# Preparation pieces of an attention kernel, split in halves over two odd slots

## The chip, the core and the metric

The kernel runs on one core of a Trainium2 chip. A core has five engines that each work through their own queue in order: TensorE (PE, matmul, with its weight loads as PEld), VectorE (DVE), ScalarE (ACT), GpSimd (POOL) and SyncE (SP, which issues DMAs). They wait for each other by semaphores. The metric is the device time of one launch in microseconds; three runs of the kernel before gave a median of 1124.78 (1123.45 to 1125.7).

## What is computed

One layer of causal attention over 2048 positions of width 512 with 16 heads of 32, and then a mixture of experts with a shared expert. All is float32. Cut to what matters here:

```python
qkv = (x @ w_qkv).reshape(B, S, 3, H, D)             # S = 2048, H = 16, D = 32
q, k, v = qkv[:, :, 0], qkv[:, :, 1], qkv[:, :, 2]
q, k = unit_norm(q), unit_norm(k)                    # per head, over D
q, k = rope_on_every_second_head(q), rope_on_every_second_head(k)
logits = einsum('bshd,bthd->bhst', q, k) * q_gain
attn = softmax(where(causal, logits, lowest))
x = layernorm(x + einsum('bhst,bthd->bshd', attn, v).reshape(B, S, Dm) @ w_out)
x = layernorm(x + experts(x))                        # top 2 of 8 experts, and a shared one
```

## The kernel before

The change lies in `fast_attention`, which takes the first 570 us. It runs under a manual schedule: every engine does its work in the order in which the Python code emits it.

**Units and slots.** The 16 heads make 4 groups g of 4 heads, the queries 4 blocks b of 512, the keys 16 tiles kt of 128. A *unit* is one (g, b, kt) with kt not behind block b: 4 + 8 + 12 + 16 = 40 units a group, 160 in all. The main loop (L518) has one *slot* n for each unit. Within a block, masked (diagonal) and whole key tiles alternate. A masked unit has 512, 384, 256 or 128 columns of queries, by its place on the diagonal; a whole one has 512. In slot n:

- `scores(n)` (L335) issues four matmuls of 32 contraction rows, one for each head of the group, into two pairs of PSUM banks. There are three pairs (`banks(1, 3, 1)`, L521), so the first pair of unit n needs the second exponential of unit n-2 done, and the second pair the first exponential of unit n-1.
- `exps(n, 0)` and `exps(n, 1)` (L350, ScalarE) read one pair each and write probabilities to one of three buffers.
- `sums(n - 1)` (L365, VectorE) adds the probabilities of the unit before to the block's sums. `causal(n)` (L358, GpSimd) masks the diagonal tile of a masked unit.
- `values(n)` (L380, TensorE) multiplies the probabilities with v into the block's one accumulator bank. It is kept back in `pending` and comes in a later slot. The last one of a block lets ScalarE copy the accumulator out (`fy`, L396).

**Other work in the slots.** The preparation of later units comes in *pieces*: `qkv(u, tl)` (L117) makes q, k and v of one tile of 128 positions for one group and block u = 4g + b. A piece has two steps, `first` (two matmuls with 128 rows and 384 columns) and `second` (two more, then two ScalarE copies, L139 and L140, out of PSUM). It needs a bank from the pool "m", which from slot 8 on is a **single bank**. The fourth piece of u starts `norm_rope(u)` (L146), whose six steps are spread over the next six slots: squares (ScalarE), lengths (VectorE), the root's seeds (ScalarE, L626 and L627), scaling (VectorE), and two rotations (VectorE and GpSimd). Then two *short steps* `qk_transposed(u, s)` (L200) turn q and k with four transposes in the same single bank and a ScalarE copy (L211). When a block ends, an *end step* (L402) adds its sums over the partitions with four matmuls (L405), again in the single bank; ScalarE copies them out (L414) and takes Ln and Exp (L415, L416), and VectorE refines and divides (L422 to L428).

**Order by slot parity**, from slot 8 to 159. In an even slot, after the scores, all pending values of earlier units are issued (as a rule two units), and one short step or an end step where one is due. In an odd slot `long_step(n)` (L452) takes the next piece and issues both its steps; the pending values wait for the next even slot. Where `rests(n)` (L477) is true, or `may_start` (L445) finds that the buffers of the next piece are not free, the odd slot goes without a piece: it then issues the values of the unit before, and the next even slot has those of one unit. A group has 20 odd slots and 16 pieces. The odd slots without a piece are 11, 21, 29 and 37 in the first group, 43, 53, 63 and 73 in the second, and 83, 93, 103 and 113 in the third. The fourth group has no pieces left to hand out after slot 127 and takes the output projections instead.

```python
for step in queue.pop(0)[1]:                     # L455, in long_step
    step()
...
if n % 2 and (rests(n) or not long_step(n)):     # L558, in an odd slot
    values_before(n)
```

## Time and profile before

| | us |
|---|---|
| runs, median of 3 | 1124.78 (1123.45 to 1125.7) |
| the profiled execution | 1121.6 |
| its span, first to last instruction | 1119.9 |
| scores of slot 0, 40, 80, 120 start at | 34.6, 175.7, 301.4, 427.7 |
| TensorE busy | 1097.1 |
| VectorE busy | 584.2 |
| ScalarE busy | 511.3 |
| GpSimd busy | 215.7 |

How to read the rows: the first number of a row of the order of time is its start in microseconds from the start of the span, the second its length, then engine, line, operation, out<-in, the shapes and the number of records put together (a matmul of this kernel leaves two records). In square brackets stands the idle time of the engine ahead of it, and what ended it. Matmuls are pipelined and their ends are modelled: the distance from one row's start to the next one's is the safer measure. In the stretches of busy times, the numbers of one row are its length and then the busy time of PE, PEld, DVE, ACT and POOL, each with its count.

### The profile page before, as it was taken

The page shows a single profiled execution, that of the slowest core. Times are in us where ns is not written, and L with a number is a line of the kernel's source. Part 1 is how long each engine was busy: PE and PEld are TensorE (multiplying, and loading weights), DVE is VectorE, ACT ScalarE, POOL GpSimd, SP SyncE. Part 2 cuts the span into 40 slices and gives each one's busy share as a digit, 9 for nine tenths or more (in the row PEclk, how much of TensorE's full clock was granted, in tenths as well). Part 3 has the DMA queues.
Part 4 walks back from the last instruction along what each step waited for, and adds up shares of the span by engine and source line. Part 5 has one row for each costly group of instructions (what it writes and reads, how often), then busy time and mean ns, then how long its engine had stood idle before and what let it go on. Part 6 is the DMA issues. An engine that isn't in the chain of part 4 may idle for free. (4 is left out here: it accounts for less than half of the span.)

```text
span 1119.9 us, 14794 instructions
## 1 busy us (share of the span) xinstructions
PE 1097.1 (98%) x5810; PEld 576.0 (51%) x5810; DVE 584.2 (52%) x771; ACT 511.3 (46%) x858; POOL 215.7 (19%) x249
## 2 busy tenths in 40 slices
PE   9999999999999999999999999999999999999997
PEld 6543333334334344333356677666665656557774
DVE  1467887787877877887865451111111111104445
ACT  3577878777877877757551100121111212111111
POOL 0221222223133221210000011111111110025441
PEclk9999999999999999999999999999999999999998
DMA  9700000000000000062112496311221211035451
GB/s 284 271 1 1 1 1 1 2 1 1 1 1 1 1 1 1 20 232 61 39 67 104 169 324 214 119 66 66 67 66 64 64 61 57 29 128 186 162 158 57
DMA packets 49539, 88.15 MB, mean 79 GB/s; under 512 B 8016, under 2 KB 22352, under 8 KB 49360
## 3 DMA queue, kind: packets, MB, share of 16 engines
q1 hardware_dynamic: 43376, 69.37, 18.2%
q0 software_dynamic: 5280, 17.31, 4.9%
q8 instruction: 49, 0.80, 0.3%
q10 hardware_dynamic: 800, 0.39, 0.1%
q14 instruction: 34, 0.28, 0.1%
HBM read 65.56 MB, written 27.79 MB: 83 GB/s over the span
## 5 line engine op out<-in xcount | busy, mean ns | idle before, releaser
L352 ACT ACTIVATE big<-fps_s,neg_gmax 128x1024 f32<-128x1024 f32 (+3 forms) x320 | 296.9, 984 | 63.8 <-PE fps_s L342 59.4
L378 DVE TENSOR_TENSOR facc<-facc,big 128x2048 f32<-128x2048 f32 (+3 forms) x128 | 248.9, 1945 | 48.1 <-ACT big L352 29.5
L126 PE MATMUL fps_qkv<-big,shared 128*128 128x384 f32 x512 | 181.0, 497 | 1.1 <-ACT big L211 0.8
L342 PE MATMUL fps_s<-big 32*128 32x512 f32 (+3 forms) x1280 | 169.3, 576 | 3.9 <-ACT big L352 2.5
L387 PE MATMUL fps_av<-big 128*32 128x512 f32 (+3 forms) x1280 | 139.7, 536 | 2.1 <-POOL big L363 1.9
L126 PEld LDWEIGHTS fps_qkv<-big,shared 128*128 128x128 f32 x512 | 92.0, 190 | 88.8 <-ACT big L211 14.9
L363 POOL TENSOR_SCALAR_AFFINE_SELECT big<-big 128x512 f32<-128x512 f32 x64 | 72.1, 1127 | 338.6 <-ACT big L352 330.5
L1048 DVE COPY xT<-ps_xT 128x512 f32<-128x512 f32 x32 | 22.1, 691 | 161.4 <-PE ps_xT L1046 161.4
L342 PEld LDWEIGHTS fps_s<-big 32*128 32x128 f32 x1280 | 54.6, 182 | 93.6 <-issue 52.1
L1079 PE MATMUL ps_dr<-big,hT 128*128 128x512 f32 (+3 forms) x240 | 93.4, 593 | 0.5 <-ACT hT L1056 0.5
L1087 ACT COPY y<-ps_dr 128x512 f32<-128x512 f32 x34 | 19.9, 586 | 157.4 <-PE ps_dr L1079 157.4
L1223 PE MATMUL ps_gr<-big,xT 128*128 128x352 f32 (+1 forms) x320 | 86.3, 460 | 0.0
L1223 PE MATMUL ps_ur<-big,xT 128*128 128x352 f32 (+1 forms) x320 | 86.2, 460 | 0.0
L1037 POOL DMA_INDIRECT rows<-x1d,rows_of x34 | 32.5, 955 | 243.3 <-PE ps_xT L1046 198.0
L679 PE MATMUL ps_us<-big,shared 128*128 128x256 f32 x336 | 78.4, 379 | 0.0
L387 PEld LDWEIGHTS fps_av<-big 128*32 128x32 f32 x1280 | 31.8, 108 | 82.7 <-issue 64.8
L1223 PEld LDWEIGHTS ps_gr<-big,xT 128*128 128x128 f32 (+1 forms) x320 | 50.3, 173 | 39.4 <-issue 18.7
L690 ACT ACTIVATE acts<-ps_gs 128x256 f32<-128x256 f32 x34 | 12.9, 379 | 124.6 <-PE ps_gs L679 124.6
L679 PEld LDWEIGHTS ps_us<-big,shared 128*128 128x128 f32 x336 | 63.8, 190 | 8.6
L679 PE MATMUL ps_gs<-big,shared 128*128 128x256 f32 x280 | 66.9, 382 | 0.0
L1004 PE MATMUL ps_ds<-shared,big 128*128 128x512 f32 x140 | 61.6, 594 | 0.6 <-DVE big L692 0.6
L1223 PEld LDWEIGHTS ps_ur<-big,xT 128*128 128x128 f32 (+1 forms) x320 | 48.0, 174 | 22.6 <-issue 2.3
(204 smaller groups left out, 1096.6 us busy)
## 6 DMA issues: line engine op xcount, KB each, us to landing
yd<-y SPq DMA_DIRECT2D x34, 256.0 KB, 2.0
big<-in_L_ffn_w_gate_dram SPq DMA_DIRECT2D x8, 704.0 KB, 10.0
big<-in_L_ffn_w_up_dram SPq DMA_DIRECT2D x8, 704.0 KB, 10.3
big<-in_L_attn_x_dram SPq DMA_DIRECT2D x16, 256.0 KB, 4.6
fres<-in_L_attn_x_dram SPq DMA_DIRECT2D x16, 256.0 KB, 3.0
x1d<-big SPq DMA_DIRECT2D x16, 256.0 KB, 2.0
big<-in_L_ffn_w_down_dram SPq DMA_DIRECT2D x8, 512.0 KB, 7.2
out_dram<-big SPq DMA_DIRECT2D x16, 256.0 KB, 2.0
```

The lines of the kernel that those rows point to most:

```text
L126: nc.tensor.matmul(ps[0], xT[:, t, c * P : (c + 1) * P], wq_sb[c].rearrange("p (s m) -> p s m", s=3)[:, :, g * P : (g + 1) * P], start=(c ...
L342: nc.tensor.matmul(pss[n][i // 2][:, i % 2, off:], k_at[(g * NB + kb) % KV][r, kl, :], q_at[u % Q][r, off:], start=True, stop=True,)
L352: nc.scalar.activation(pr_at[n % PR][:, 2 * j : 2 * j + 2, off:], pss[n][j][:, :, off:], AF.Exp, bias=neg_gmax)
L363: nc.gpsimd.affine_select(d, d, [[0, 4], [1, P]], ALU.is_ge, 0.0, base=0, channel_multiplier=-1)
L378: nc.vector.tensor_tensor(acc[:, :, off:], first[:, :, off:], pr[:, :, off:], ALU.add)
L387: nc.tensor.matmul(avs[g, b][32 * i : 32 * i + 32, off:], v_at[(g * NB + kb) % KV][:, kl, i * HD : (i + 1) * HD], pr_at[n % PR][:, i, off: ...
L679: nc.tensor.matmul(ps.rearrange("p (t m) -> p t m", t=BT), w[:, c, lo : lo + P], x[:, :, c, :], start=(c == 0), stop=(c == NC - 1),)
L1004: nc.tensor.matmul(pd, hid[:, j, tl * P : (tl + 1) * P], wd[:, j, :], start=(j == 0), stop=False)
L1037: nc.gpsimd.indirect_dma_start(r, None, x1d, bass.IndirectOffsetOnAxis(ap=rows_of[:, i : i + 1], axis=0))
L1048: nc.any.tensor_copy(xT, pst)
L1079: nc.tensor.matmul(pd[slots, :], hT[:w, c, slots], big[:w, bass.ds(at_d + (DOWNS + c * DM), DM)], start=(c == 0), stop=(c == NHC - 1),)
L1223: nc.tensor.matmul(ps[slots, :], xT[:, c, slots], big[:, bass.ds(at_e + (at + c * HE), HE)], start=(c == 0), stop=(c == NC - 1),)
```

## The change

`rests` becomes `halved`, which names other slots, and `long_step` gets a flag. Where an odd slot is halved, `long_step` issues only the first step of the next piece and keeps the second in `held`; the next call issues that step and nothing else. While a step is held, the even slot between the two issues neither a short step nor an end step, since the single bank is occupied. No odd slot rests any more by rule.

```diff
+        held = []
+
-        def long_step(n):
+        def long_step(n, half=False):
+            if held:
+                held.pop()()
+                return True
             if not queue or not may_start(queue[0][0], n):
                 return False
-            for step in queue.pop(0)[1]:
-                step()
+            steps = queue.pop(0)[1]
+            steps[0]()
+            if half:
+                held.append(steps[1])
+            else:
+                steps[1]()
...
-        def rests(n):
+        def halved(n):
             at = n % (NU // NC)
-            return n < NU - NU // NC and at in ((3, 13, 23, 33) if n >= NU // NC else (11, 21, 29, 37))
+            return n < NU - NU // NC and at in ((3, 11, 21, 31) if n >= NU // NC else (9, 21, 29, 37))
...
-                        if masked and not ending:
+                        if masked and not ending and not held:
                             short_step(n)
                         values_before(n)
-                        end_step(n)
-                        if not masked and not ending:
+                        if not held:
+                            end_step(n)
+                        if not masked and not ending and not held:
                             short_step(n)
...
-                    if n % 2 and (rests(n) or not long_step(n)):
+                    if n % 2 and not long_step(n, halved(n)):
                         values_before(n)
```

The order of TensorE's work in the two programs, slot by slot, differs in this. Pieces now stand in halves in slots 9 and 11, 21 and 23, 37 and 39 of the first group, in 43 and 45, 51 and 53, 61 and 63, 71 and 73 of the second, and in 83 and 85, 91 and 93, 101 and 103, 111 and 113 of the third: eleven pieces. Slot 29 still goes without, since `may_start` refuses there, and slot 31 has its whole piece as before. The values that stood in the odd slots 11, 21, 37, 43, 53 and so on now stand in the even slot behind, two units together. One short step moves from slot 38 to slot 40. Every other slot has the work that it had, and the fourth piece of every block ends in the same slot as before.

## The prediction

> **What bounds the kernel now.** I read the page's busy times first, then the busy times by stretch, then TensorE's order of time where it stops, and last what it waits for.

> ```profile
> span 1119.9 us, 14794 instructions
> PE 1097.1 (98%) x5810; PEld 576.0 (51%) x5810; DVE 584.2 (52%) x771; ACT 511.3 (46%) x858; POOL 215.7 (19%) x249
> ```

> ```profile
> core 0: us, PE busy (x) PEld busy (x) DVE busy (x) ACT busy (x) POOL busy (x), PEclk, DMA share, GB/s
> 176.00:301.00 125.00, 123.70 (x828) 48.38 (x820) 100.30 (x86) 99.26 (x147) 34.36 (x28) 1.00 0.00 1
> 301.00:427.00 126.00, 124.70 (x833) 49.03 (x832) 100.85 (x85) 99.85 (x148) 34.28 (x28) 1.00 0.00 1
> ```

> TensorE is the bound: 98% of the span, 99% in the second and third group of heads (the two stretches), at clock 1.00 and with no DMA. But a busy row hides waits, since its ends are modelled. So I compare distances between the starts of rows (each matmul is two records, so x8 is four). A score unit of 512 columns normally takes 1.07 us to the next start, one of 128 columns 0.43, a whole piece of preparation 2.78, values of two units 1.74 ahead of sums and 1.85 ahead of scores. Slot 44 of the second group, behind the odd slot 43 that has no piece, is different:

> ```profile
> 185.36 0.50 PE L342 MATMUL fps_s<-big 32*128 32x128 f32 x8
> 185.79 0.64 PE L387 MATMUL fps_av<-big 128*32 128x256 f32 x8
> 186.36 1.13 PE L342 MATMUL fps_s<-big 32*128 32x512 f32 x4
> 188.20 1.13 PE L342 MATMUL fps_s<-big 32*128 32x512 f32 x4 [0.71 <-ACT big L352]
> 189.27 0.43 PE L387 MATMUL fps_av<-big 128*32 128x128 f32 x8
> 189.63 1.14 PE L342 MATMUL fps_s<-big 32*128 32x512 f32 x8
> 190.70 2.85 PE L126 MATMUL fps_qkv<-big,shared 128*128 128x384 f32 x8
> 193.48 0.93 PE L342 MATMUL fps_s<-big 32*128 32x384 f32 x8
> ```

> The scores of unit 44 take 2.91 us (186.36 to 189.27) instead of 1.07: 1.84 lost, though only 0.71 shows as idle. Their second half waits for a pair of banks that the exponentials of unit 43 must empty (188.20), and the values at 189.27 wait for the mask of unit 43. ScalarE and GpSimd say why:

> ```profile
> 185.50 0.59 ACT L414 COPY facc<-fps_sum 128x512 f32<-128x512 f32 x1 [1.24 <-PE fps_sum L405]
> 186.12 0.63 ACT L415 ACTIVATE frec<-facc 128x512 f32<-128x512 f32 x1
> 186.78 0.63 ACT L416 ACTIVATE frec<-frec 128x512 f32<-128x512 f32 x1
> 187.69 2.83 ACT L352 ACTIVATE big<-fps_s,neg_gmax 128x256 f32<-128x256 f32 x4
> ```

> ```profile
> 188.58 0.64 POOL L363 TENSOR_SCALAR_AFFINE_SELECT big<-big 128x512 f32<-128x512 f32 x1 [3.62 <-ACT big L352]
> ```

> ScalarE normalizes a finished block for 2 us ahead of exps(43), and TensorE has only 1.0 us of work for that time. The same happens, smaller, behind the other odd slots without a piece, for instance 53:

> ```profile
> 216.20 1.19 PE L342 MATMUL fps_s<-big 32*128 32x512 f32 x8
> 217.97 1.06 PE L387 MATMUL fps_av<-big 128*32 128x512 f32 x8 [0.58 <-POOL big L363]
> 218.96 1.09 PE L342 MATMUL fps_s<-big 32*128 32x384 f32 x8
> 219.98 1.21 PE L387 MATMUL fps_av<-big 128*32 128x512 f32 x8
> ```

> **The change part by part.** No instruction is added or removed and no DMA is moved. A whole piece costs 2.78 us where it stands behind scores and 2.68 behind transposes (slots 0 to 5), so a half is 1.34 and 0.10 for the change from scores: 1.44. Each split thus costs 0.10, eleven 1.1 us in all. Against it, values of two units cost 1.99 in two places (1.00 and 0.99) and 1.85 in one, so each closed odd slot returns 0.14 where TensorE is not waiting.
> [...]

> *Slots 43 to 45 (and 83 to 85).* The first half takes the single bank, which the sums of the finished block leave at 186.09 (L414's end); I take 186.2, so it ends at 187.64 with the change of mode. PE's queue behind it is scores(44), whose first pair moves from 186.36 to 187.64, but the second pair can't start before 188.20 anyway: scores end at 188.74. Now values(42), 0.46, fill the time to the mask (189.22), values(43) run from 189.27 and scores(45) start at 189.63, as before. From there a half replaces the whole: scores(46) at 189.63 + 1.07 + 1.44 = 192.14 instead of 193.48. Gain 1.34. exps(45) ends at 193.02 and exps(46) needs VectorE's sums of unit 43 (end 194.2), so ScalarE gets some 0.15 less, within its idle 1.1 us there. Bounds: 0.88 if values(42) add their 0.46 behind the mask, 1.85 if no wait is left.

> *Slots 51 to 54 (91 to 94).* Nominal times after: 51 is 2.51 (1.07 + 1.44), 52 stays 2.29, 53 is 2.51, 54 is 3.57: 10.88, against 11.92 (210.06 to 221.98). The masked values(52) no longer stand in slot 53. ScalarE's queue (exps(52), copy of the finished block 0.46, seeds 0.42, exps(53) 2.1) lets scores(54) start their second pair 0.1 late. Gain 0.9; bounds 0.2, if the two copies of the piece (0.65), which now fall behind exps(53), push exps(54) and the sums by as much, and 1.04.

> *Slots 61 to 64 (101 to 104).* 2.51 + 2.93 + 2.51 + 2.93 = 10.87 against 11.18: 0.31. *Slots 71 to 74 (111 to 114).* 2.51 + 2.29 + 2.51 + 2.93 = 10.23 against 10.63: 0.40. Waits there are ScalarE's, 0.3 us each, and a unit's TensorE time (2.5 to 2.9) now exceeds its two exponentials (2.1) everywhere. VectorE works without a pause from 280 to 300, but that stretch begins with the sums of unit 72, whose scores now come 1.3 earlier. Bounds 0 and the same figures.

> *First group.* Slots 21 to 24: 10.87 against 11.28, gain 0.40 (0.3 by VectorE's fixed chain from 116.84). Slots 37 to 40: 11.46 against 11.76 gives 0.30, but a transposing step moves from slot 38 to 40, where its copy now queues behind the block's copy, and the piece of slot 41 waits some 0.35 for the bank: 0 (bounds -0.35 and 0.30). Slot 29 is unchanged: nothing may start there. Slots 9 to 13: exps(12) start at 87.75, when VectorE has finished the sums of unit 9, a chain that began before slot 9; then the copies follow and the piece of slot 13 gets its bank at 90.89, as now:

> ```profile
> 90.89 2.85 PE L126 MATMUL fps_qkv<-big,shared 128*128 128x384 f32 x8 [0.84 <-ACT big L211]
> ```

> Gain 0 (bounds -0.1 and the 2.1 of all waits there).

> Sum: 2 x (1.34 + 0.90 + 0.31 + 0.40) + 0.40 = 6.3 us. Bounds: 2 x (0.88 + 0.2) + 0.3 - 0.35 - 0.1 = 2.0, and 2 x 3.60 + 0.4 + 0.3 + 2.1 = 10.0. The profiled execution took 1121.6 us (span 1119.9); it becomes 1115.3. The median of the runs is 3.2 above it, so 1124.8 becomes 1118.5. Pieces end in the same slots as before, so the fourth group, the projections and the experts only start earlier.

> **The rivals.**
> *ScalarE paces the block changes.* Both large waits end on ScalarE. If it is full there, slots 43 and 53 and their twins give nothing: 2 x 0.71 + 0.4 = 1.8 left, 1123.0. For it: it works without a pause from 185.5 to 193; against it: 21% idle over the group (99.26 busy of 125), and 1.1 us idle ahead of the next sums (197.24).
> [...]
> *All waits go,* the first group's at slots 11 to 13 too: 10.0, 1114.8. Against it stands VectorE's chain at 87.66.
> *The held bank costs more than the slots give: slower.* A half-done piece keeps the only single bank for two slots. If each of the eleven first halves waits for it as the piece at 90.89 did, 0.84, with scores queued behind and ScalarE then starved, that is 9.2 - 6.3 = 2.9 us slower, 1127.7; it decides from 0.57 a piece. Against it: only one step is moved to another slot, and at nine of the eleven places the last copy out of the bank lies before the first half's place (copies end at 167.5 for the one at 167.9 in slot 37); at 43 and 83 it is 0.4 late, in time that is lost anyway.

> **How the numbers follow.** Forecast 0.58; a part of it (some 4 us, 1120.8) 0.07; ScalarE paces 0.15; all waits go 0.12; slower 0.08. Differences under 0.2% (2.2 us) can't be told from none. Faster 0.77, same 0.15, slower 0.08. The likeliest case alone spans 1116.6 to 1119.9 (8.2 to 4.9 us). The range adds the rival at 1123.0, and a microsecond below, as the three runs differ by 2.3: 1115.5 to 1123.2.

> **What would show it.** Right: scores(44) and (84) without the 1.8 us, the distance from slot 42 to 47 1.3 shorter, each of the middle groups (125.7 and 126.3 from scores 40 to 80 and 80 to 120) some 3 us shorter, slots 9 to 14 unchanged. Wrong: PE rows waiting on L139, L140 or L211 behind a first half, exps behind sums on VectorE in slots 71 to 78, or groups of the old length with ScalarE busier.

## The result, and the profile after

The changed kernel took 1118.98 us (median of 11 runs, 1116.75 to 1122.08), the kernel before beside it 1124.08 (11 runs, 1119.94 to 1125.76): a ratio of 0.9961 [0.9947, 0.9974], 0.39% or 4.4 us. Timed again beside the experiments it took 1117.20 against 1124.02, a ratio of 0.9945 [0.9933, 0.9957]. Its profiled execution took 1119.15 us with a span of 1117.4, against 1121.6 and 1119.9.

So the forecast of 1118.5 us was met, in part by luck. Its sum was not: it forecast 6.3 us from the slots, and the slots gave 3.5. The rest came from something that the prediction doesn't mention, and whose cause stays in part open.

The page's busy times after, and the busy times of the stretches of the second and third group (columns as in the prediction: length, then PE, PEld, DVE, ACT and POOL, then the granted clock):

```profile
span 1117.4 us, 14796 instructions
PE 1096.7 (98%) x5810; PEld 575.2 (51%) x5810; DVE 585.9 (52%) x771; ACT 510.3 (46%) x858; POOL 208.9 (19%) x249
```

```profile
176.00:301.00 125.00, 124.73 (x840) 48.98 (x840) 103.30 (x86) 99.95 (x150) 30.84 (x28) 1.00 0.00 1
301.00:427.00 126.00, 125.73 (x848) 49.09 (x840) 102.33 (x86) 100.91 (x150) 30.81 (x28) 1.00 0.00 1
```

TensorE's total stays, as no work was taken out; the idle time in the stretches falls from 1.3 us to 0.3 in each. The groups themselves, from scores(40) to (80) and from (80) to (120), went from 125.69 and 126.32 us to 124.78 each: 0.91 and 1.54 shorter, where the prediction named some 3 us each as a sign of being right. The first gains less since the transposing step that left slot 38 now stands in slot 40. The busy rows, which fall alike in both stretches, don't tell this, so distances are read again. Scores of slots, from start to start, in us:

| slots | before | after | gain | forecast |
|---|---|---|---|---|
| 9 to 14 | 15.70 | 15.69 | 0.01 | 0 |
| 21 to 25 | 11.27 | 11.01 | 0.26 | 0.40 |
| 37 to 42 | 15.39 | 15.18 | 0.21 | 0 |
| 42 to 47, 82 to 87 | 14.83 each | 13.96 each | 0.87 each | 1.34 each |
| 51 to 55, 91 to 95 | 11.92, 11.93 | 11.33 each | 0.59, 0.60 | 0.90 each |
| 61 to 65, 101 to 105 | 11.18, 11.17 | 11.30, 11.31 | -0.12, -0.14 | 0.31 each |
| 71 to 75, 111 to 115 | 10.64, 10.66 | 10.46 each | 0.18, 0.20 | 0.40 each |
| 0 to 120 | 393.06 | 389.54 | 3.52 | 6.3 |

Every distance between these slots agrees within 0.02 us. Behind slot 120 the distances are alike too (120 to 130 takes 35.10 in both), but for slot 138, where a transpose waits for data that a DMA brings (after, TensorE idles 2.79 ahead of it, on an addition of VectorE that waits 2.95 for the DMA): 4.64 before, 5.31 after, and 4.3 to 6.2 over all the profiles of this study, without a pattern. In these two profiles the gain of 3.52 shrinks to a span shorter by 2.5, since slot 0 starts 0.36 later and slot 138 takes 0.67 longer.

TensorE in the largest place, slots 43 to 46 of the second group (start, length, engine, line, operation; the answer to the rows 185.36 to 193.48 of before):

```profile
185.25 0.50 PE L342 MATMUL fps_s<-big 32*128 32x128 f32 x8
186.02 1.56 PE L126 MATMUL fps_qkv<-big,shared 128*128 128x384 f32 x4 [0.27 <-ACT facc L414]
187.51 1.71 PE L342 MATMUL fps_s<-big 32*128 32x512 f32 x8
189.15 0.86 PE L387 MATMUL fps_av<-big 128*32 128x256 f32 x16
189.94 1.14 PE L342 MATMUL fps_s<-big 32*128 32x512 f32 x8
191.01 1.56 PE L126 MATMUL fps_qkv<-big,shared 128*128 128x384 f32 x4
192.49 0.93 PE L342 MATMUL fps_s<-big 32*128 32x384 f32 x8
```

The first half of the piece (186.02) fills the time ahead of scores(44), as forecast; the wait on L414 in front of it shows 0.27. But scores(44) start at 187.51 and hold TensorE until 189.15: 1.64 instead of 1.07. A wait of 0.57 is left. ScalarE says for what:

```profile
187.58 0.82 ACT L352 ACTIVATE big<-fps_s,neg_gmax 128x256 f32<-128x256 f32 x2
```

The first exponential of unit 43 empties the pair of banks about half of 0.82 behind 187.58, and the second pair of scores(44) takes 1.07 us from there. Slots 53 and 54, where before TensorE stood idle for 0.58, and slot 62:

```profile
215.13 1.56 PE L126 MATMUL fps_qkv<-big,shared 128*128 128x384 f32 x4
216.61 1.15 PE L342 MATMUL fps_s<-big 32*128 32x384 f32 x8
217.69 1.92 PE L387 MATMUL fps_av<-big 128*32 128x512 f32 x16
...
242.11 1.48 PE L342 MATMUL fps_s<-big 32*128 32x512 f32 x8
243.52 1.92 PE L387 MATMUL fps_av<-big 128*32 128x512 f32 x16
```

Slot 53 has a half (215.13) in place of the masked values, and no wait. Scores(54), of 384 columns, take 1.08 to the next start where 0.86 is the normal distance: 0.22 of waiting. Scores(62) take 1.41 instead of 1.07, and 61 to 65 thus became longer than before. From slot 9 to 14 the time stayed, with the same 0.84 ahead of the whole piece of slot 13. But the wait now stands in one place: before, scores(11) waited 0.82 (83.68 to 85.57, less 1.07) and slot 13 had 1.16 (88.66 to 90.89, less 1.07); after, slot 13 alone has 1.99 (88.18 to 91.24, less 1.07). Before, and after:

```profile
83.68 1.14 PE L342 MATMUL fps_s<-big 32*128 32x512 f32 x8
85.57 0.42 PE L387 MATMUL fps_av<-big 128*32 128x128 f32 x8 [0.75 <-POOL big L363]
...
88.66 1.39 PE L342 MATMUL fps_s<-big 32*128 32x512 f32 x8
```

```profile
88.18 2.22 PE L342 MATMUL fps_s<-big 32*128 32x512 f32 x8
91.24 2.85 PE L126 MATMUL fps_qkv<-big,shared 128*128 128x384 f32 x8 [0.84 <-ACT big L211]
```

### The profile page after: what moved, and what is told of

Read it like the earlier page. It is cut to its first block, busy times and chain, and to the rows that moved or that the text cites. A ratio compares the mean times of both kernels' runs of the same rounds, so it can differ in the third digit from the quotient of the medians.

```text
span 1117.4 us, 14796 instructions
## 1 busy us (share of the span) xinstructions
PE 1096.7 (98%) x5810; PEld 575.2 (51%) x5810; DVE 585.9 (52%) x771; ACT 510.3 (46%) x858; POOL 208.9 (19%) x249
## 5 line engine op out<-in xcount | busy, mean ns | idle before, releaser
L352 ACT ACTIVATE big<-fps_s,neg_gmax 128x1024 f32<-128x1024 f32 (+3 forms) x320 | 297.3, 984 | 65.7 <-PE fps_s L342 61.0
L126 PE MATMUL fps_qkv<-big,shared 128*128 128x384 f32 x512 | 184.0, 499 | 1.7 <-ACT facc L414 0.8
L342 PE MATMUL fps_s<-big 32*128 32x512 f32 (+3 forms) x1280 | 168.3, 576 | 2.5 <-ACT big L211 1.4
L126 PEld LDWEIGHTS fps_qkv<-big,shared 128*128 128x128 f32 x512 | 91.1, 189 | 93.6 <-issue 20.3
L387 PE MATMUL fps_av<-big 128*32 128x512 f32 (+3 forms) x1280 | 137.1, 535 | 0.2 <-ACT big L352 0.2
L363 POOL TENSOR_SCALAR_AFFINE_SELECT big<-big 128x512 f32<-128x512 f32 x64 | 65.4, 1021 | 345.8 <-ACT big L352 337.2
L342 PEld LDWEIGHTS fps_s<-big 32*128 32x128 f32 x1280 | 54.0, 182 | 90.1 <-issue 51.2
L387 PEld LDWEIGHTS fps_av<-big 128*32 128x32 f32 x1280 | 32.6, 109 | 78.5 <-issue 63.6
```

The lines of the kernel that those rows point to most:

```text
L126: nc.tensor.matmul(ps[0], xT[:, t, c * P : (c + 1) * P], wq_sb[c].rearrange("p (s m) -> p s m", s=3)[:, :, g * P : (g + 1) * P], start=(c ...
L342: nc.tensor.matmul(pss[n][i // 2][:, i % 2, off:], k_at[(g * NB + kb) % KV][r, kl, :], q_at[u % Q][r, off:], start=True, stop=True,)
L352: nc.scalar.activation(pr_at[n % PR][:, 2 * j : 2 * j + 2, off:], pss[n][j][:, :, off:], AF.Exp, bias=neg_gmax)
L363: nc.gpsimd.affine_select(d, d, [[0, 4], [1, P]], ALU.is_ge, 0.0, base=0, channel_multiplier=-1)
L387: nc.tensor.matmul(avs[g, b][32 * i : 32 * i + 32, off:], v_at[(g * NB + kb) % KV][:, kl, i * HD : (i + 1) * HD], pr_at[n % PR][:, i, off: ...
```

## The experiments

Two things had to be explained: why the slots gave 3.5 us and not 6.3, and where the measured time beyond 3.5 came from. The theory for the first: a split costs more than 0.10, and a wait is left at the places where ScalarE still empties banks. Its rival: VectorE or a longer ScalarE queue holds the units back. Distances in the trace repeat within 0.02 us where the granted clock is 1.00, so one profile tells a change of 0.1 us; medians do not.

**One split undone, at slots 43 and 83.** The odd slot rests again, a whole piece stands in 45 and 85; all other halves stay.

```diff
-  return n < NU - NU // NC and at in ((3, 11, 21, 31) if n >= NU // NC else (9, 21, 29, 37))
+  return n < NU - NU // NC and at in ((11, 21, 31) if n >= NU // NC else (9, 21, 29, 37))
+def rests(n):
+  return NU // NC <= n < NU - NU // NC and n % (NU // NC) in (3,)
...
-  if n % 2 and not long_step(n, halved(n)):
+  if n % 2 and (rests(n) or not long_step(n, halved(n))):
```

> Undoes the halving at slots 43/45 and 83/85 alone: slots 43 and 83 go without a piece again, 45 and 85 have a whole one. Theory (a half gains what it fills of a wait on ScalarE, and costs its own entry): from scores(42) to scores(47) the distance goes back from 13.96 us in the changed kernel to the 14.83 of the kernel before, in both groups, 1.75 us in all, and no other distance moves. Rival (an even load gains wherever an odd slot is closed, some 0.3 us a place): the distance grows by 0.3 only.

Slots 82 to 87 took 14.83, what they take in the kernel before, with every other distance as in the changed kernel: the 0.87 belong to this one split. Slots 42 to 47, with the same order of work, took 16.43. The busy times of the stretch there (the granted clock is the last number but two) and TensorE's rows show where the 1.60 between them come from:

```profile
189.00:193.00 4.00, 4.00 (x20) 1.60 (x17) 3.93 (x5) 3.25 (x5) 2.81 (x3) 0.57 0.00 0
```

```profile
189.23 2.09 PE L342 MATMUL fps_s<-big 32*128 32x512 f32 x8
191.25 3.50 PE L126 MATMUL fps_qkv<-big,shared 128*128 128x384 f32 x8
```

Right behind the restored wait of 1.84 the granted clock is 0.57 over 4 us, and the same rows that took 1.14 and 2.85 take 2.09 and 3.50. By its records the clock was 0.5 from 189.2 to 192.6. That is the first hint for the second question. The run took 1120.04, the kernel before beside it 1123.97.

**One split undone, at slots 63 and 103.** The same edit with 21 taken out of the halved slots and a rest at 23.

```diff
-  ... at in ((3, 11, 21, 31) if n >= NU // NC else (9, 21, 29, 37))
+  ... at in ((3, 11, 31) if n >= NU // NC else (9, 21, 29, 37))
+  rests(n): NU // NC <= n < NU - NU // NC and n % (NU // NC) in (23,)
```

> Undoes the halving at slots 61/63 and 101/103 alone: a whole piece in 61 and 101, none in 63 and 103. Theory (no wait worth filling stands there, and the split costs 0.2 us of entry into 128-row work): from scores(61) to scores(65) 11.18 us as in the kernel before, 0.12 shorter than the 11.30 of the changed kernel. Rival (every closed odd slot gains, as the prediction had it, 0.31): the distance would have to grow over 11.30.

Slots 61 to 65 and 101 to 105 went back to 11.17: the split there costs 0.13 where the prediction had a gain of 0.31. Slots 9 to 14, which the edit doesn't touch, took 17.37 instead of 15.69, with a clock of 0.5 from 91.9 to 95.3, behind the wait of slot 13:

```profile
91.90:95.30 3.40, 3.40 (x6) 1.89 (x7) 1.46 (x1) 1.83 (x2) 0.32 (x1) 0.50 0.00 0
```

```profile
88.72 2.21 PE L342 MATMUL fps_s<-big 32*128 32x512 f32 x8
91.77 4.54 PE L126 MATMUL fps_qkv<-big,shared 128*128 128x384 f32 x8 [0.84 <-ACT big L211]
```

The piece that takes 2.85 elsewhere took 4.54. The run took 1120.31.

**ScalarE's queue at the end of a block.** To see if the two passes Ln and Exp ahead of exps(43) are what keeps scores(44) waiting, they are issued one slot later, and VectorE's refinement with them, in all groups but the last.

```diff
-                nc.scalar.activation(rec, den, AF.Ln)
-                nc.scalar.activation(rec, rec, AF.Exp, scale=-1.0)
-                later(1 if g < NC - 1 else 2, lambda: refine(rec, den))
+                def inverse():
+                    nc.scalar.activation(rec, den, AF.Ln)
+                    nc.scalar.activation(rec, rec, AF.Exp, scale=-1.0)
+                if g < NC - 1:
+                    later(1, inverse)
+                    later(2, lambda: refine(rec, den))
+                else: ...
```

> Changed kernel, but ScalarE takes Ln and Exp of a finished block's sums one slot later, behind the exponentials of the next unit, and VectorE refines one slot later; the fourth group stays as it is. Theory (at slots 43 and 44 TensorE waits for exps(43), which stand behind these two, 1.3 us): scores(44) lose their wait of 0.57, and from scores(42) to scores(47) it takes 13.3 to 13.6 us instead of 13.96; the 0.34 that the first half waits for the bank stay. Rival (the mask or the bank sets slot 44): 13.9 to 14.0.

A miss: 42 to 47 took 13.93 instead of 13.96. That is the rival's time, but not by the rival's cause, as TensorE's rows in that place tell:

```profile
191.42 1.14 PE L342 MATMUL fps_s<-big 32*128 32x512 f32 x8
192.49 0.86 PE L387 MATMUL fps_av<-big 128*32 128x256 f32 x16
193.28 1.67 PE L342 MATMUL fps_s<-big 32*128 32x512 f32 x8
194.88 1.56 PE L126 MATMUL fps_qkv<-big,shared 128*128 128x384 f32 x4
```

Scores(44) no longer wait (1.07 from 191.42 to 192.49), but scores(45) now do: 1.60 from 193.28, a wait of 0.53, since they need the exponentials of 44, which now stand behind Ln and Exp. The wait moved by one unit and kept its size, so it is ScalarE's order of work by which it stands, and moving 1.3 us of that work by a slot doesn't cure it. In the first group the edit did harm: 0 to 9 took 0.98 longer, and 9 to 14 took 18.71 with a stretch of half clock at 94.0. The run took 1122.43.

**The chain of VectorE in slots 9 to 13.** The prediction held that this place gives nothing because VectorE is late. The six steps of `norm_rope` of the last early block, which come two a slot there, are spread over six slots, and its transposes come five slots later.

```diff
-  for what, k in zip(steps, (0, 0, 1, 1, 2, 2) if u < NB else (1, 2, 3, 4, 5, 6)):
+  for what, k in zip(steps, (0, 0, 1, 1, 2, 2) if u < NB - 1 else (1, 2, 3, 4, 5, 6)):
...
-  shorts.append((now[0] + (3 if u < EARLY else 4 if u < NB else 9), qk_transposed(u, s), u))
+  shorts.append((now[0] + (3 if u < EARLY else 4 if u < NB - 1 else 9), qk_transposed(u, s), u))
```

> Changed kernel, but the six steps of the preparation of block 3 of the first group are spread over slots 8 to 13 as those of later groups are, instead of standing in slots 7 to 9, and its transposes come later. Theory (slots 9 to 14 gain nothing from the half since exps(12) wait for VectorE's chain that began before slot 9): with the chain gone the wait of 2.0 us in slot 13 goes, and from scores(9) to scores(20) it takes 33.3 to 33.9 us instead of 35.53. Rival (ScalarE's copies and the single bank hold slot 13): 35.0 or more.

Slots 9 to 14 took 13.46 instead of 15.69, 9 to 20 33.89 instead of 35.53, 0 to 120 387.90 instead of 389.54. VectorE's chain in the changed kernel, and TensorE's rows in slot 13 of this one:

```profile
85.30 5.91 DVE L378 TENSOR_TENSOR facc<-facc,big 128x2048 f32<-128x2048 f32 x3
```

```profile
87.88 1.21 PE L342 MATMUL fps_s<-big 32*128 32x512 f32 x8
89.02 2.85 PE L126 MATMUL fps_qkv<-big,shared 128*128 128x384 f32 x8
```

Three sums run in one piece from 85.30 to 91.21 there; with the steps spread they no longer pile up, exps(12) start at 86.79 right behind ScalarE's copies instead of at 88.11, and the piece follows the scores at 89.02 without the 0.84. That VectorE's chain held exps(12), the prediction's reason for the zero, is shown. But the edit also moves the transposes out of slot 12, and with them the copy (L211) that the 0.84 ended on, so the parts of the chain and of the single bank in the gain aren't told apart. Slots 14 to 20 became longer, 20.43 instead of 19.85. This run took 1116.66 us.

**Is that version faster in the time?** The changed kernel and this version, timed side by side.

> The changed kernel once more, beside the kernel before on the same chip. From scores(0) to scores(120) 389.5 us (before: 393.1), each distance as in its first profile within 0.05, unless a stretch of half clock lies in it. Theory of the spread (a window of 3.4 us in which TensorE has waited much lets the next 3.4 us run at half clock, some 1.7 us lost, and where the windows fall is chance): the mean granted clock of the runs falls on a few values, 0.998, 0.996 and 0.994 or so, and the time rises by 1.5 to 2 us from one to the next; the kernel before has more runs at the low values. Rival (the spread is DMA's or the launch's): time and clock are unrelated.

> The version with block 3 of the first group spread, timed. Theory: 1.6 us shorter than the changed kernel from its places, and up to 1 us more since the long wait in slot 13, one of those that can bring half clock, is gone: median 1116 to 1117.5, fewer runs at clock 0.994. Rival (the gap of slots 9 to 13 is only moved, and comes back in the fourth group): the median of the changed kernel.

The changed kernel took 1117.20 (1116.68 to 1120.37; ratio to before 0.9945 [0.9933, 0.9957]), the spread version 1117.47 (1117.15 to 1118.92; 0.9943 [0.9931, 0.9956]). The changed kernel's times follow the mean clock, as its theory had it (1116.68 to 1117.28 us at 0.997 and 0.998, 1118.60 at 0.996, 1120.37 at 0.994); those of the spread version don't (1117.15 and 1118.92 both at 0.997). Its 0 to 120 is again shorter by 1.61 (387.92 against 389.53), but in its profile slot 0 started 1.02 later (35.94 against 34.92). So it is shorter than both kernels from slot 0 to 120, and the time can't tell it from the changed one. The 3.4 us in the theory of the spread is the length of the stretches at slots 44 and 13 above (189.2 to 192.6, 91.9 to 95.3); that the waiting counts over a window as long was the author's guess when it was put on record, and the last section has what the profiles show of it.

**All that seemed good, together.** The spread steps, the rest at slots 63 and 103, and in slots 43, 83 and 123 the values of the unit before ahead of the half, to let the bank come free in the meantime.

```diff
+                    if n > NU // NC and n % (NU // NC) == 3:
+                        values_before(n)
-                    if n % 2 and not long_step(n, halved(n)):
+                    if n % 2 and (rests(n) or not long_step(n, halved(n))):
                         values_before(n)
```

> Spread block 3, no piece in slots 63 and 103 (a whole one in 61 and 101), and in slots 43, 83 and 123 the values that are pending stand ahead of the piece, where it waits for the bank. Theory (the first half waits 0.34 us there for the bank, which values of 0.46 fill, and scores(44) then come when exps(43) are done): from scores(42) to (47) 13.4 to 13.6 us instead of 13.96, (61) to (65) 11.18 instead of 11.30, (9) to (20) 33.9, (0) to (120) 386.5 to 387; median 1114.5 to 1116.5. Rival (the mask of unit 43 holds slot 44, whatever stands ahead of it): (42) to (47) 13.9 to 14.0.

A miss in the third part: 42 to 47 and 82 to 87 took 14.15 and 14.17, 0.2 more than in the changed kernel. The half no longer waits for its bank, but scores(44) still wait 0.35, and scores(45) now 0.64. The other two parts held (61 to 65 back at 11.17, 9 to 14 at 13.45). 0 to 120 took 388.05 and the runs 1118.17 (1117.89 to 1119.01; ratio 0.995 [0.9938, 0.9963]), above the forecasts for both and no better than the changed kernel.

**TensorE kept busy in slot 13.** For the second question: four multiplications with the identity on either side of scores(13), into banks that are overwritten later.

```diff
+            if n == 13:
+                keep_busy(pss[n][0][:, 0, :], 4)
...
+                    if n == 13:
+                        early[14] = [pools["s"].tile([P, 2, QB], F32, tag="s", name="fps_s14_0")]
+                        keep_busy(early[14][0][:, 0, :], 4)
```

> The changed kernel with eight useless matmuls of the identity, 128 columns each, in slot 13: four ahead of scores(13) and four behind them, into banks that are overwritten later; they fill time in which TensorE waits. Theory of the spread: the distance from scores(9) to (14) stays 15.7 to 15.9, and no stretch of half clock begins in slots 13 to 15; the runs have fewer at clock 0.994 than the changed kernel's. Rival (half clock has another cause): as many as in the changed kernel.

Inconclusive. Slots 9 to 14 took 15.68, and the profile shows no half clock in the attention. But the mean granted clocks of the five runs were 0.998, 0.997 and three times 0.995, no higher than those of the changed kernel, and the median was 1120.16 (1117.17 to 1121.31).

**The wait doubled, and the doubled wait filled.** A clearer test of the same, on the kernel before: seven extra squares on ScalarE ahead of exps(43) and exps(83) lengthen the wait of slots 44 and 84; in the second kernel TensorE has 16 multiplications with the identity to do in that time.

```diff
                     scores(n)
+                    if n in (43, 83):
+                        for _ in range(7):
+                            nc.scalar.activation(junk, ident, AF.Square)
                     exps(n, 0)
```

> The kernel before, with seven useless ScalarE squares of 128x128 (some 0.27 us each) ahead of exps(43) and exps(83): the wait of TensorE at scores(44) and (84) grows from 1.84 to 3.7 us. Theory (little work on TensorE through a window of 3.4 us brings half clock in the next): stretches of half clock follow both places, from scores(42) to (47) and from (82) to (87) it takes 16.7 us and up to 1.7 more, and all runs have a mean clock below 0.994. Rival (half clock has another cause, such as the launch or DMA): 16.7 us, and the clocks of the kernel before.

```diff
+            if n in (44, 84):
+                keep_busy(pss[n][0][:, 0, :], 16)
             for i in range(4):
```

> The same, with sixteen useless matmuls of the identity, 128 columns each, ahead of scores(44) and (84), into a bank that the scores overwrite: the wait is as long, but TensorE works through most of it. Theory: 16.7 to 17.2 us from scores(42) to (47) and from (82) to (87), no half clock there, the mean clocks at 0.994 to 0.998 and the median 2 to 4 us below the kernel with the wait left empty. Rival: the same as with the wait left empty.

The busy times by stretch with the granted clock, and TensorE in slot 44, in the kernel with the doubled wait:

```profile
189.00:196.00 7.00, 5.44 (x22) 1.75 (x23) 4.77 (x8) 5.10 (x10) 3.05 (x5) 0.52 0.00 0
```

```profile
186.47 1.13 PE L343 MATMUL fps_s<-big 32*128 32x512 f32 x4
190.56 2.08 PE L343 MATMUL fps_s<-big 32*128 32x512 f32 x4 [2.96 <-ACT big L353]
```

And with the wait filled (L1541 is the helper that issues the multiplications with the identity; its rows overlap the time that the wait had):

```profile
189.00:196.00 7.00, 6.70 (x46) 4.12 (x46) 5.13 (x9) 6.23 (x13) 2.75 (x4) 1.00 0.00 0
```

```profile
187.06 3.84 PE L1541 MATMUL fps_s<-ident 128*128 128x128 f32 x32
190.83 1.44 PE L345 MATMUL fps_s<-big 32*128 32x512 f32 x8
```

With TensorE idle the clock falls to half, at both places, for 6.83 us each by its records (189.25 to 196.08 and 322.37 to 329.20); 42 to 47 and 82 to 87 take 19.62 and 20.35, more than the forecast of 16.7 and up to 1.7; each stretch is twice as long as the theory had it. With TensorE busy over the same time the clock stays at 1.00, and both take 17.72, 0.5 over the forecast. The same wait thus costs 1.9 and 2.6 us more when TensorE idles in it. The runs took 1132.97 (1130.29 to 1134.02; ratio 1.0078 [1.0056, 1.01]) and 1131.05 (1130.21 to 1131.43; 1.0062 [1.0044, 1.008]); their mean clocks were 0.990 to 0.992 and 0.994 to 0.995. So the median with the wait filled lies 1.9 us lower, just short of the forecast, but its clocks are no higher than those of the kernel before beside it (0.994 and 0.995 in five of six runs). Its profile has a stretch of half clock in the attention all the same, from 504.51, behind slot 138, where TensorE idles for 3.24 until data has come.

## Why the prediction was right, and its sum too large

**The bound and the places: right.** TensorE is the bound, and the gain lies first at 43 to 45, then at 51 to 54. Undoing the one split gave back 0.87. Slots 9 to 13 gave nothing, and exps(12) were held there by VectorE's chain, as the spread steps showed. Pieces end in the same slots, and everything from slot 120 on only starts earlier.

**Half a piece at 1.44, a split at 0.10: mis-sized.** A half takes 1.48 to 1.49 from its start to the next row's (215.13 to 216.61, 186.02 to 187.51). Two halves are 2.97 against 2.78 for a whole piece: about 0.20 a split, not 0.10. The whole piece behind transposes, from which the 0.10 was read, thus has half of such a cost in it too. Over eleven splits that is some 1.1 us. Where TensorE waits anyway, as in slots 9 to 13, it costs nothing (9 to 14 took 15.70 before and 15.69 after). The prediction calls its 0.10 a change of mode at slot 43; no run shows a mode, only the distances: about 0.20 for one more step from scores of 32 rows into a piece of 128. What these are made of, no run tells.

**"Scores end at 188.74": the step that failed at slots 43 to 45.** The prediction let the second pair of scores(44) start at 188.20 and end half a unit later. It takes its whole 1.07 from the start, late or not; the kernel before shows just that, 188.20 to 189.27, in lines that stand in the prediction. The four heads of a unit run beside each other: two alone take 1.07 there, as four do behind them (189.63 to 190.70), so a pair that starts late gains nothing from the first being done. Against the start of slot 43, scores(45) were forecast at 4.27 and came at 4.69; of the 0.47 missing, 0.42 are this and 0.04 the second half's price.

**"A unit's TensorE time (2.5 to 2.9) now exceeds its two exponentials (2.1) everywhere": the step that failed at slots 51 to 74.** A mean over a unit doesn't tell whether the pair of banks is free when the scores start. By distances, scores(52) and (72) keep 0.13 of waiting, scores(54) 0.22, scores(62) 0.34. With the 0.57 at scores(44) and 0.34 in front of the half of slot 43 (this one was foreseen) each middle group keeps some 1.7 us of waits. That is why 61 to 65 became slower, and the rests the better choice there, by 0.13. The rival that ScalarE paces the block changes was true in part (the late Ln and Exp only moved the wait from scores(44) to scores(45)); but its price, nothing gained at 43 and 53, is refuted by 0.87 and 0.59. That all waits go is refuted by slot 13 and by the 1.7 us left.

**Slots 37 to 40 at 0: too low.** The wait of 0.35 for the bank behind the moved transposing step did not come; 0.30 less 0.10 for the dearer split is the 0.21 seen. **The held bank** cost little: ahead of a first half the trace shows an idle time only in slots 43 and 83, some 0.3 us each, where the bank waits for the block's copy as forecast, and the rival's 0.84 at eleven places is refuted.

**Why the time fitted all the same: two errors that cancel.** "The median of the runs is 3.2 above it" was carried over to the changed kernel without a reason. There the profiled execution became 2.45 us shorter (1121.6 to 1119.15) and not 6.3, and the median of 1118.98 lies 0.2 below it and not 3.2 above. The first makes the forecast 3.9 us too low and the second 3.4 too high, which leaves the 0.5 by which it missed. That they cancel is luck.

With 3.5 us from the slots, the kernels beside which it was timed (1124.08 and 1124.02) would give some 1120.5; 1118.98 and 1117.20 were measured, 1.6 and 3.3 less. The prediction read the clock as 1.00 and left it at that. The granted clock has stretches at 0.5, 3.41 us long or twice that. A stretch of 3.41 us cost 1.60 at slot 44 and 1.68 at slot 13 above, and lowers a run's mean clock by 0.0015 (half of 3.41 in 1118). The profiles of the kernels before and after have none in the attention, and one each in the experts (from 997.97 and from 995.28; ten of the twelve profiles have one there). Every profile ends in one more, behind TensorE's last work, where it costs TensorE nothing and lowers the mean clock by 0.0016 to 0.0030; so a mean clock tells the number of the others only roughly. Those in the attention came behind long waits of TensorE: that the doubled wait (2.96 of idle time at slot 44) brings them at slots 44 and 84, and the same wait filled does not, is shown. The change took the wait of 1.84 away at two places, and none of 0.57 was followed by such a stretch in any profile; but it gathered the waits of slots 11 and 13 into one of 1.99, and those of slot 13 were followed by one in two of five profiles. It agrees that of 19 runs of the kernel before whose mean clock was recorded 16 have 0.995 or less, and of 17 of the changed kernel 5. At equal clock the two kernels lie 2 to 3 us apart, about what the slots give: spans of 1120.0 and 1119.9 against 1116.9 to 1117.4 at 0.996, and 1117.9 against 1114.8 to 1115.9 at 0.998. The missing 1.6 to 3.3 us would then be one or two stretches of half clock that the changed kernel meets less often.

That last step is argued from the mean clocks, not shown, and one run speaks against slots 44 and 84 as the place. With their wait filled no stretch follows there, yet the clocks of all four runs stayed at 0.994 and 0.995, and the median lies 7.4 us above the kernel before beside it (1131.05 against 1123.60), of which the way from slot 0 to 120 accounts for 5.8 (398.85 against 393.06). The profile of the kernel before has none of these stretches behind slot 44 or 84; the experiment that restored the wait has one, at one of two places. How often the kernel before meets them at which slot stays open, and the attempt to remove them from slot 13 showed nothing.

## What to carry to other kernels

When a piece of work is split to fill waits, price the half by its own distance from start to start, and ask for each row behind it whether its banks are free at its start: an average share of busy time doesn't answer that. Here a row of heads that run beside each other ended its full 1.07 us after the last of them had started. Waits of TensorE of 1.84 to 2.4 us were followed by half the clock in three of nine cases, and the one of 1.84 then cost 1.60 more than itself, so a change that removes such a wait should be judged by distances in the trace and by the runs' mean clock, each by itself.
